# The queries' maxima over keys: four TensorE transposes, or VectorE's block transpose, one small TensorE transpose and a block diagonal from GpSimd

## The chip, the core and the metric

The kernel runs on one core of a Trainium2 chip. The metric is the device time of one launch in microseconds. The kernel before was run three times: 2422.80, 2423.19 and 2423.44 us, median 2423.19.

## The reference

Four sequences of 2048 tokens with 512 features, all in fp32, go through one layer: attention with one head of width 512, then a sparse feed-forward part.

```
q, k, v = relu(norm(x) @ Wq + bq), relu(norm(x) @ Wk + bk), relu(norm(x) @ Wv + bv)
e = q @ k.T / sqrt(512) - 10000 * (key is later than query)
e = exp(e - max(e, axis=keys))            # the maximum that this change is about
y = (e / sum(e, axis=keys)) @ v
x = x + norm(relu(y @ Wo + bo))
x = x + norm(feed_forward(norm(x)))       # top 32 of 512 outputs and of 512 inputs per token
```

## The kernel before

**Two phases.** Phase 1 is the attention, phase 2 the feed-forward part. Phase 1 works on groups of 512 queries (`GT`), four groups in each of four sequences, 16 in all, so that group `j` is group `j % 4` of its sequence. A group needs the keys of its own group and of those before it in the sequence. The program also holds a second form of both phases for inputs with large scores (`every_key=True`); with these inputs it isn't executed.

**Scores with keys on the partitions.** A score tile `st` holds 128 keys on its partitions and the group's 512 queries in its free dimension. `n.mx` (128 x 512, shown as `mxsum`) is the running maximum over all score tiles, made on VectorE by `combine` (line 227) as tiles come in. At the end `n.mx` still has 128 partial maxima for each query, one on each partition.

**The fold.** The maximum of each query over these 128 partitions must be found, and laid on every partition, since it is subtracted from score tiles that have keys on the partitions. Three functions do it:

- `fold` (713 to 718): four TensorE transposes of 128x128 put the queries on the partitions, in PSUM.
- `diagonals` (726 to 731): `reduced` (720 to 724) takes the maximum over the free dimension on VectorE, 128 queries x 4 tiles; then four VectorE scalings of the identity by one column each make four diagonal matrices, `n.dg`, 128 x 512.
- `spread` (733 to 736): a matmul of a matrix of ones with `n.dg` lays each query's maximum on all 128 partitions, `n.mb` in PSUM (128 x 512).

`weights` (738 to 752) then subtracts `n.mb` from each score tile (VectorE, 744), takes the exponential (ScalarE, 745) and adds up the tiles (GpSimd, 747 and 749). `attend` (774) multiplies the tiles with the values.

**The seven products.** Projections, and scores against the keys of earlier groups, are done as Strassen products of 2x2 blocks: class `Seven` (529), with the methods `p1` to `p7`, each four fp32 matmuls of 128x256 (line 561, two passes each in the profile). `p2`, `p3` and `p5` are copied out by ScalarE (580); `p1`, `p6` and `p7` leave a sum that VectorE evicts (609 and 613), and the next product of the same accumulator comes after that eviction. The letters name the target: `V`, `Q`, `K`, `O` for values, queries, keys and outputs of the next group, `A` and `N` for scores against earlier keys.

**The order of the work.** In phase 1 the order of the instructions on TensorE, VectorE and GpSimd is the order in which the program issues them; on ScalarE and SP (the DMA queue) it is left to the framework. TensorE's order is written out in `steps` (927). VectorE's jobs are put between TensorE's by the class `Pace` (229): it keeps an estimate of the time of TensorE (`pace.pe(us)`) and VectorE, and takes the next ready job from three ranks, lowest rank first; `pace.flush(job)` issues what is left of a job at once. The estimates only decide the order. Around the fold `steps` reads:

```
V.p3(), V.p6()
pace.flush(*n.maxima)
...
tp = fold(n.mx)
dg = pace.add(0, work(1.8, diagonals, n, tp))
pace.pe(0.45)
if last:
    next(filler), next(filler)
else:
    Q = Seven(nxt, "q")
    Q.p2(), Q.p5(), V.p7(), Q.p1(), V.p4()
pace.flush(dg)
spread(n)
```

In the last group there is no next one; its place is taken by `filler`, the products of `bound` (876 to 899, lines 886 and 898), which belong to a check on the size of the scores. The job list also holds `key_sums` (496), which stores key blocks by SP, `moments` (302), whose inverse root is GpSimd's (line 139), and `chain` (802), the norms of the group before.

**Buffers.** `n.dg` is a tile named `xn` of the pool `two`, which has two buffers for that name; `turn_x` (340) uses the same two later in the group. Weight loads go through a ring of 13 buffers (`Ring`, 357).

Of the kernel before, what the change touches and what calls it, by code (L numbers as in the profile page):

```python
# [28 lines left out]
F32 = mybir.dt.float32  # L29
# [3 lines left out]
ALU = mybir.AluOpType  # L33
AX = mybir.AxisListType
# [5 lines left out]
P = 128  # L40
GT = 512
TPG = GT // P
# [7 lines left out]
BLK = 32  # L50
# [3 lines left out]
def sandwich_kernel(ctx: ExitStack, tc: tile.TileContext, io: dict, out: bass.AP):  # L54
    nc = tc.nc
# [18 lines left out]
    ident = const.tile([P, P], F32, name="ident")  # L74
# [5 lines left out]
        out=causal, in_=causal, pattern=[[1, P]], compare_op=ALU.is_ge, fill=neg_raw, base=0, channel_multiplier=-1  # L80
    )
    ones = const.tile([P, P], F32, name="ones")
# [118 lines left out]
    def phase1(every_key):  # L201
# [8 lines left out]
        sm = enter("sm", 4)  # L210
        two = enter("two", 2)
# [70 lines left out]
        pace = Pace()  # L282
        ends = []

        def work(us, fn, *args, pause=0.0):

            fn(*args)
            yield us, pause
# [13 lines left out]
        def moments(n, joint=True):  # L302

            n.rstd = sm.tile([P, TPG], F32, name="rstd_x")
            var = sm.tile([P, TPG], F32, name="var_x")
            n.mv = sm.tile([P, TPG, nc.vector.BN_AGGR_DIM], F32, name="mv_x")
            for t, xt in enumerate(n.x):
                st = sm.tile([P, nc.vector.BN_STATS_DIM], F32, name="st_x")
                nc.vector.bn_stats(st, xt)
                nc.vector.bn_aggr(n.mv[:, t, :], st)  # L310
                if not joint:
                    nc.vector.tensor_scalar_add(var[:, t : t + 1], n.mv[:, t, 1:2], LN_EPS)
                    inv_sqrt(n.rstd[:, t : t + 1], var[:, t : t + 1])
                yield 0.8, 0.0
            if joint:
                nc.vector.tensor_scalar_add(var, n.mv[:, :, 1], LN_EPS)  # L316
                inv_sqrt(n.rstd, var)
                yield 0.2, (0.55,)
                n.shift = sm.tile([P, TPG], F32, name="shift_x")
                combine(n.shift, n.mv[:, :, 0], n.rstd, ALU.mult, -1.0)  # L320
                yield 0.2, 0.5

        def at_once(pieces):
            for _ in pieces:
                pass
# [14 lines left out]
        def turn_x(n):  # L340

            for t in range(TPG):
                xn = two.tile([P, D], F32, name="xn")
                nc.scalar.activation(
                    xn, n.x[t], AF.Identity, scale=n.rstd[:, t : t + 1], bias=n.shift[:, t : t + 1]
                )
                yield 0.0, 1.0
                nc.vector.transpose(n.x[t], xn)
                nc.sync.dma_start(xnT_d[n.i][t * P : (t + 1) * P, :], n.x[t])
                yield 0.65, 0.0  # L350
# [6 lines left out]
        class Ring:  # L357
# [36 lines left out]
            def drop(self, i):  # L394
                self.gone.add(i)
                self.fill()
# [313 lines left out]
            n.nk = GB * TPG if every_key else (n.g + 1) * TPG  # L710
            n.st, n.mx, n.maxima = [None] * n.nk, None, []

        def fold(src):

            tp = ps_tp.tile([P, NC, P], F32, name="tp")
            for t in range(TPG):
                nc.tensor.transpose(tp[:, t, :], src[:, t * P : (t + 1) * P], ident)
            return tp

        def reduced(tp, op):  # L720

            r = sm.tile([P, TPG], F32, name="fold")
            nc.vector.tensor_reduce(r, tp, axis=AX.X, op=op)
            return r

        def diagonals(n, tp):

            m = reduced(tp, ALU.max)
            n.dg = two.tile([P, TPG, P], F32, name="xn")
            for t in range(TPG):  # L730
                nc.vector.tensor_scalar_mul(n.dg[:, t, :], ident, m[:, t : t + 1])

        def spread(n):

            n.mb = ps_mm.tile([P, GT], F32, name="mm")
            nc.tensor.matmul(n.mb, lhsT=ones, rhs=n.dg.rearrange("p t q -> p (t q)"), start=True, stop=True)  # L736

        def weights(n):

# [136 lines left out]
        def bound():  # L876

            w = ring.take("q", range(NC))  # L880
            for d in range(NC):
                ps = ps_mm.tile([P, GT], F32, name="mm")

                cols = slice(d * P, D)
                for c in range(NC):
                    nc.tensor.matmul(
                        ps[:, cols],
                        lhsT=w[c][1][:, d * P : (d + 1) * P],
                        rhs=w[c][1][:, cols],
                        start=(c == 0),  # L890
                        stop=(c == NC - 1),
                    )
                    if c % 2:
                        pace.pe(0.43 * (NC - d))
                    if c == 1:
                        yield
                sqr = prp.tile([P, D], F32, name="pr")
                nc.scalar.activation(sqr[:, cols], ps[:, cols], AF.Square, accum_out=squared[:, 0, d : d + 1])
                yield
# [27 lines left out]
        def steps(n, ahead):  # L927
# [3 lines left out]
            for j in range(NGRP):  # L931
                nxt = ahead
                last = nxt is None
                filler = bound() if last else None
# [45 lines left out]
                else:  # L980
                    V = Seven(nxt, "v")
# [14 lines left out]
                stored = pace.add(1, key_sums(n)) if n.g < GB - 1 else None  # L996
                if ahead is not None:
                    measured = pace.add(1, moments(ahead), 2.0)
                tp = fold(n.mx)
                dg = pace.add(0, work(1.8, diagonals, n, tp))  # L1000
                pace.pe(0.45)
                if last:
                    next(filler), next(filler)
                else:
                    Q = Seven(nxt, "q")
                    Q.p2(), Q.p5(), V.p7(), Q.p1(), V.p4()
                pace.flush(dg)
                spread(n)
                pace.pe(0.86)
# [9 lines left out]
                if ahead is not None:  # L1019
                    pace.flush(measured)  # L1020
                    turned = pace.add(1, turn_x(ahead))
# [52 lines left out]
                before, n = n, nxt  # L1074
# [4 lines left out]
        n = load(*order[0], queues=(nc.sync, nc.sync if every_key else nc.scalar))  # L1079
# [15 lines left out]
        if every_key:  # L1095
            bo = broadcast(wp, "L0_attn_bo")
            for b in range(B):
                kTs, vos = [], []
                for g in range(GB):
                    if b + g:  # L1100
                        n = load(b, g)
                        at_once(moments(n))
                    transpose_x(n)
                    drop(project(n, "v"))
                    drop(project(n, "k"))
                    drop(project_vo(n))
                    kTs.append(n.kT)
                    vos.append(n.vo)
                for g in range(GB):
                    n = load(b, g)  # L1110
                    at_once(moments(n))
                    transpose_x(n)
                    drop(project(n, "q"))
                    no_scores(n)
                    for kt in range(n.nk):
                        score_tile(n, kt, kTs[kt // TPG])
                    diagonals(n, fold(n.mx))
                    spread(n)
                    at_once(weights(n))
                    inverses(n, summed(n.sum))  # L1120
                    n.a, n.xg, n.xr = [None] * TPG, [None] * TPG, [None] * TPG
                    for t in range(TPG):
                        load_residual(n, t)
                        attended(n, t, attend(n, t, vos))
                        at_once(chain(n, t))
                        if n.i == NGRP - 1 and t < TPG - 1:
                            features(n, t)
                    if n.i < NGRP - 1:
                        fetch_features(n.i)
                        pace.drain()  # L1130
            for br in branches:
                first_moments(n, br)
            ends.append(n.xg[TPG - 1])
        else:

            transpose_x(n)
            ahead = load(*order[1])
            at_once(moments(ahead))
            for m in "vqk":
                w = project(n, m)  # L1140
                weight_sums(m, w)
                if m == "k":
                    squares(w)
                drop(w)
            w = project_vo(n)
            ahead.ahead = [normed(ahead, t) for t in range(2)]
            weight_sums("o", w)
            drop(w)
            head.close()

            bo = broadcast(wp, "L0_attn_bo")
            for br in branches:
                nc.gpsimd.dma_start(
                    conv_w[br],
                    io[f"L0_ffn_{br}_conv_w"].rearrange("g f -> (g f)").rearrange("(o n) -> o n", o=1).broadcast_to((P, D)),
                )
            with tc.manual_schedule(engines={PE, mybir.EngineType.DVE, mybir.EngineType.Pool}):
                steps(n, ahead)
# [375 lines left out]
```

## Time and profile before

| | |
|---|---|
| median of three runs | 2423.19 us |
| the profiled execution, its time | 2423.45 us |
| its span in the profile | 2421.7 us |
| its granted TensorE clock | 0.996 |
| TensorE / VectorE / ScalarE / GpSimd busy | 98% / 74% / 46% / 38% |
| fold, TensorE transposes (717) | 64, 273 ns each |
| fold, VectorE reduction (723) | 16, 681 ns each |
| fold, VectorE scalings (731) | 64, 282 ns each |
| spread, TensorE matmul passes (736) | 32, 594 ns each |

A profile row names line, engine, operation, output<-input and shapes, the number of instructions, then their busy time and the mean of one, and the engine's idle time before them with what ended it. `PEld` is TensorE's weight load, which runs beside its matmuls. A matmul's duration in the profile includes its way through the array, so matmuls that follow each other overlap; what one costs in a stream is the distance from its start to the next one's.

### The profile page before, as it was taken

How to read it: one execution, taken by the hardware profiler on the slowest of the kernel's cores; microseconds unless marked ns; L12 is line 12 of the kernel's file. 1: busy time of each engine (PE TensorE's matmuls, PEld its weight loads, DVE VectorE, ACT ScalarE, POOL GpSimd, SP SyncE). 2: the span in 40 equal slices, each digit the busy share in tenths (PEclk: the TensorE clock that was granted, in tenths of full speed). 3: DMA queues.
4: the chain of work that ended last, by engine and by line, in shares of the span. 5: the costliest groups of instructions: out<-in, count | busy, mean ns of one | idle time of the engine just before them, and what ended most of it. 6: DMA issues, size and time to landing. Idle time of an engine off the chain costs nothing.

```text
span 2421.7 us, 29446 instructions
## 1 busy us (share of the span) xinstructions
PE 2368.4 (98%) x8418; PEld 1526.3 (63%) x8418; DVE 1788.8 (74%) x3879; ACT 1117.2 (46%) x2352; POOL 929.8 (38%) x875
## 2 busy tenths in 40 slices
PE   8999999999999999999999999999989999999997
PEld 3776858587685857768585776857434444444443
DVE  2588675558866565887656678655599999999997
ACT  2333423233442233343223334322268888888886
POOL 1012210311221031121203112120379999999997
PEclk9999999999999999999999999999999999999999
DMA  6587756568875656887565677734334444444441
GB/s 218 181 243 202 209 168 171 142 183 222 225 213 151 176 138 184 215 233 213 143 185 135 185 212 219 213 100 126 94 82 98 114 122 114 122 114 122 113 122 54
DMA packets 594735, 392.18 MB, mean 162 GB/s; under 512 B 393090, under 2 KB 460162, under 8 KB 594564
## 3 DMA queue, kind: packets, MB, share of 16 engines
q1 hardware_dynamic: 590932, 386.53, 57.6%
q10 hardware_dynamic: 3312, 2.63, 0.3%
q8 instruction: 70, 1.15, 0.2%
q0 software_dynamic: 320, 1.05, 0.2%
q14 instruction: 101, 0.83, 0.1%
HBM read 275.26 MB, written 114.82 MB: 161 GB/s over the span
## 4 chain that ended last, share of the span: by engine, by line
PE 73%; DVE 15%; ACT 4%; issue 4%; POOL 2%; DMA 1%; SPq 0%; POOLq 0%; ACTq 0%; DVEq 0%
PE acc L561 24%; PE acc L779 18%; PE mm L561 18%; PE mm L679 6%; DVE m_si L1246 4%; DVE m_so L1246 3%; DVE rest_so L1254 2%; DVE rest_si L1254 2%; PE mm L1325 2%; PE mm L414 2%; DVE rest_si L1257 1%; DVE rest_so L1257 1%; PE lg L1239 1%; PE mm L663 1%; PE mm L736 1%
## 5 line engine op out<-in xcount | busy, mean ns | idle before, releaser
L779 PE MATMUL acc<-vo,st 128*128 128x512 f32 x1088 | 476.0, 593 | 1.0 <-ACT st L745 1.0
L779 PEld LDWEIGHTS acc<-vo,st 128*128 128x128 f32 x1088 | 205.3, 190 | 240.4 <-issue 234.8
L1325 PE MATMUL mm<-w_L_ffn_weight,xsT 128*128 128x512 f32 x512 | 233.6, 599 | 4.1 <-ACT xsT L167 2.8
L1325 PE MATMUL mm<-w_L_ffn_weight,xnT 128*128 128x512 f32 x512 | 230.4, 592 | 1.7 <-ACT xnT L167 1.7
L139 POOL TENSOR_TENSOR rs_a<-ve_a,neg_half 128x1 f32<-128x1 f32 x64 | 44.5, 696 | 417.1 <-DVE ve_a L148 416.2
L1325 PEld LDWEIGHTS mm<-w_L_ffn_weight,xsT 128*128 128x128 f32 x512 | 98.0, 192 | 128.0 <-issue 116.2
L139 POOL TENSOR_TENSOR rstd_x<-var_x,neg_half 128x4 f32<-128x4 f32 (+1 forms) x19 | 17.8, 934 | 417.3 <-DVE var_x L316 412.7
L1325 PEld LDWEIGHTS mm<-w_L_ffn_weight,xnT 128*128 128x128 f32 x512 | 97.1, 190 | 122.9 <-issue 113.6
L561 PE MATMUL acc<-T,wb 128*128 128x256 f32 x720 | 170.2, 379 | 0.5 <-DVE qT L613 0.5
L561 PE MATMUL mm<-xnT,wb 128*128 128x256 f32 x720 | 170.1, 379 | 0.0
L749 POOL TENSOR_TENSOR mxsum<-mxsum,st 128x512 f32<-128x512 f32 (+2 forms) x144 | 162.3, 1127 | 14.6 <-ACT st L745 4.2
L561 PE MATMUL acc<-xnT,wb 128*128 128x256 f32 x720 | 165.2, 379 | 0.0
L561 PEld LDWEIGHTS acc<-T,wb 128*128 128x128 f32 x720 | 136.7, 190 | 25.9 <-issue 6.7
L561 PEld LDWEIGHTS acc<-xnT,wb 128*128 128x128 f32 x720 | 136.8, 190 | 25.0 <-issue 6.2
L561 PEld LDWEIGHTS mm<-xnT,wb 128*128 128x128 f32 x720 | 135.3, 190 | 24.0 <-issue 7.2
L679 PE MATMUL mm<-qT,kT 128*128 128x128 f32 (+3 forms) x512 | 148.6, 433 | 0.0
L227 DVE SCALAR_TENSOR_TENSOR mxsum<-mxsum,st 128x512 f32<-128x512 f32 (+2 forms) x144 | 86.5, 601 | 66.4 <-ACT st L607 61.7
L580 ACT COPY cp<-mm 128x512 f32<-128x512 f32 x72 | 42.1, 585 | 193.0 <-PE mm L561 191.8
L1246 DVE MAX8 m_si<-rest_si 128x8 f32<-128x512 f32 x192 | 129.9, 677 | 0.1
L1246 DVE MAX8 m_so<-rest_so 128x8 f32<-128x512 f32 x192 | 128.4, 669 | 0.1
L1254 DVE MATCH_REPLACE8 rest_si<-m_si,rest_si 128x512 f32<-128x512 f32 x192 | 128.4, 669 | 0.0
L1254 DVE MATCH_REPLACE8 rest_so<-m_so,rest_so 128x512 f32<-128x512 f32 x192 | 128.4, 669 | 0.0
(248 smaller groups left out, 4907.0 us busy)
## 6 DMA issues: line engine op xcount, KB each, us to landing
wb<-keys SPq DMA_DIRECT2D x168, 256.0 KB, 2.9
xr<-in_L_attn_x_dram SPq DMA_DIRECT2D x64, 256.0 KB, 3.8
x<-x SPq DMA_DIRECT2D x64, 256.0 KB, 3.1
xn<-xn SPq DMA_DIRECT2D x64, 256.0 KB, 2.9
out_dram<-h SPq DMA_DIRECT2D x64, 256.0 KB, 2.1
xt<-in_L_attn_x_dram SPq DMA_DIRECT2D x62, 256.0 KB, 3.3
wb<-Z_v SPq DMA_DIRECT2D x60, 256.0 KB, 2.9
wb<-Z_q SPq DMA_DIRECT2D x60, 256.0 KB, 3.3
```

Of the source, the lines that this page charges most:

```text
L139: nc.gpsimd.tensor_tensor(dst, src, neg_half[:, : src.shape[1]], ALU.pow)
L227: nc.vector.scalar_tensor_tensor(out, a, factor, b, ALU.mult, op)
L414: nc.tensor.matmul(ps, lhsT=w[c][1][:, d * P : (d + 1) * P], rhs=xnT[:, c, :], start=(c == 0), stop=(c == NC - 1))
L561: nc.tensor.matmul(ps[:, d * H : (d + 1) * H], lhsT=left[:, c, d * P : (d + 1) * P], rhs=right[:, c, :], start=(new and c + d == 0), stop= ...
L580: nc.scalar.copy(t, ps)
L679: nc.tensor.matmul(ps[:, off:], lhsT=kT[:, c, k : k + P], rhs=n.qT[:, c, off:], start=(c == 0), stop=(c == NC - 1),)
L749: nc.gpsimd.tensor_tensor(n.sum[:, off:], n.sum[:, off:], w, ALU.add)
L779: nc.tensor.matmul(acc, lhsT=n.st[kt][:, t * P : (t + 1) * P], rhs=vos[kt // TPG][:, kt % TPG, :], start=(kt == 0), stop=(kt == nk - 1),)
L1246: nc.vector.max(n.m8[br], n.rest[br] if k else n.lg[br])
L1254: nc.vector.match_replace(n.rest[br], n.m8[br], n.rest[br], -LOWEST)
L1257: nc.vector.match_replace(n.rest[br], n.m8[br], n.lg[br], -LOWEST)
L1325: nc.tensor.matmul(ps, lhsT=lhsT[:, c, :], rhs=wf[:, c, :], start=(c == 0), stop=(c == NC - 1))
```

## The change

The fold is done in four steps. VectorE transposes each 32x32 block of `n.mx` (`turned`), so that within each of the four block rows a partition stands for one query modulo 32, and 32 neighbouring elements are 32 keys' maxima for it. A VectorE reduction over these gives `n.m16`, 128 x 16. One TensorE transpose turns it to 16 x 128 in PSUM, a row for each block of 32 queries, and a second VectorE reduction over the four rows of blocks gives the maxima `m`, 16 x 32. GpSimd's select writes a 16 x 512 tile that has row `b`'s 32 maxima in columns `32 b` to `32 b + 31` and zeros elsewhere. The spread multiplies it with 16 rows of ones. In `steps` the first two steps are a job of their own; `Q.p2` (in the last group the first half of the filler) is issued before the TensorE transpose instead of after it, and the rest behind it.

```diff
-        def fold(src):
+        NB = GT // BLK
+
+        def block_maxima(n):
+
+            turned = two.tile([P, GT], F32, name="xn")
+            nc.vector.transpose(turned, n.mx)
+            n.m16 = sm.tile([P, NB], F32, name="m16")
+            nc.vector.tensor_reduce(n.m16, turned.rearrange("p (b k) -> p b k", k=BLK), axis=AX.X, op=ALU.max)
+
+        def fold(n):
 
             tp = ps_tp.tile([P, NC, P], F32, name="tp")
-            for t in range(TPG):
-                nc.tensor.transpose(tp[:, t, :], src[:, t * P : (t + 1) * P], ident)
-            return tp
-
-        def reduced(tp, op):
-
-            r = sm.tile([P, TPG], F32, name="fold")
-            nc.vector.tensor_reduce(r, tp, axis=AX.X, op=op)
-            return r
+            nc.tensor.transpose(tp[0:NB, 0, :], n.m16, ident)
+            return tp[0:NB, 0, :]
 
         def diagonals(n, tp):
 
-            m = reduced(tp, ALU.max)
-            n.dg = two.tile([P, TPG, P], F32, name="xn")
-            for t in range(TPG):
-                nc.vector.tensor_scalar_mul(n.dg[:, t, :], ident, m[:, t : t + 1])
+            m = sm.tile([NB, BLK], F32, name="m32")
+            nc.vector.tensor_reduce(m, tp.rearrange("b (i q) -> b q i", q=BLK), axis=AX.X, op=ALU.max)
+            n.dg = two.tile([P, GT], F32, name="xn")[0:NB, :]
+            nc.gpsimd.affine_select(
+                out=n.dg.rearrange("b (c q) -> b c q", q=BLK),
+                in_=m.unsqueeze(1).broadcast_to((NB, NB, BLK)),
+                pattern=[[1, NB], [0, BLK]],
+                compare_op=ALU.is_equal,
+                fill=0.0,
+                base=0,
+                channel_multiplier=-1,
+            )
 
         def spread(n):
 
             n.mb = ps_mm.tile([P, GT], F32, name="mm")
-            nc.tensor.matmul(n.mb, lhsT=ones, rhs=n.dg.rearrange("p t q -> p (t q)"), start=True, stop=True)
+            nc.tensor.matmul(n.mb, lhsT=ones[0:NB, :], rhs=n.dg, start=True, stop=True)
...
-                tp = fold(n.mx)
-                dg = pace.add(0, work(1.8, diagonals, n, tp))
-                pace.pe(0.45)
+                blocks = pace.add(0, work(1.4, block_maxima, n))
                 if last:
-                    next(filler), next(filler)
+                    next(filler)
                 else:
                     Q = Seven(nxt, "q")
-                    Q.p2(), Q.p5(), V.p7(), Q.p1(), V.p4()
+                    Q.p2()
+                pace.flush(blocks)
+                tp = fold(n)
+                dg = pace.add(0, work(0.3, diagonals, n, tp))
+                pace.pe(0.12)
+                if last:
+                    next(filler)
+                else:
+                    Q.p5(), V.p7(), Q.p1(), V.p4()
                 pace.flush(dg)
                 spread(n)
```

More of the change, by code (lines that the diff above doesn't have):

```diff
@@ L1116, in phase1 @@
                         score_tile(n, kt, kTs[kt // TPG])
-                    diagonals(n, fold(n.mx))
+                    block_maxima(n)
+                    diagonals(n, fold(n))
                     spread(n)
```

## The prediction

> **What bounds the kernel now.** I read the page first (busy shares, then the chain that ended last), then the windows, to see which stage the change lies in, then the timeline around one fold, then single rows for prices.
>
> ```profile
> PE 2368.4 (98%) x8418; PEld 1526.3 (63%) x8418; DVE 1788.8 (74%) x3879; ACT 1117.2 (46%) x2352; POOL 929.8 (38%) x875
> PE 73%; DVE 15%; ACT 4%; issue 4%; POOL 2%; DMA 1%; SPq 0%; POOLq 0%; ACTq 0%; DVEq 0%
> ```
>
> TensorE is busy for nearly the whole span, and most of the chain is its own matmuls. The next answer is the window of the sixteen attention groups.
>
> ```profile
> 80.00:1700.00 1620.00, 1617.27 (x6444) 1196.58 (x6443) 1079.23 (x2188) 546.54 (x1083) 294.21 (x313) 1.00 0.65 184
> ```
>
> In these 1620 us TensorE idles 2.7 us in all, VectorE 541 us, GpSimd 1326 us. So here a microsecond taken from TensorE's stream is a microsecond off the time, a microsecond in which it waits is one on it, and work of VectorE or GpSimd is free unless TensorE waits for it. All sixteen folds lie here (89.9 to 1686.4 us). One of them, group 3, in the timeline:
>
> ```profile
> 406.81 1.70 PEld L561 LDWEIGHTS acc<-T,wb 128*128 128x128 f32 x8
> 407.02 1.89 PE L561 MATMUL acc<-T,wb 128*128 128x256 f32 x8
> ...
> 408.54 0.58 PEld L717 LDWEIGHTS tp<-ident,mxsum 128*128 128x128 f32 x4
> 408.75 0.60 PE L717 MATMUL tp<-ident,mxsum 128*128 128x128 f32 x4
> ...
> 409.02 0.69 DVE L613 TENSOR_TENSOR vT<-acc,x 128x512 f32<-128x512 f32 x1 [2.76 <-PE acc L561]
> ...
> 409.19 1.89 PE L561 MATMUL mm<-xnT,wb 128*128 128x256 f32 x8
> 409.63 0.68 DVE L723 TENSOR_REDUCE fold<-tp 128x4 f32<-128x512 f32 x1
> ...
> 410.35 0.87 DVE L731 TENSOR_SCALAR xn<-ident,fold 128x128 f32<-128x128 f32 x4
> ...
> 411.14 0.68 DVE L309 BATCH_NORM_STATS2 st_x<-xt 128x6 f32<-128x512 f32 x1
> ```
>
> The line from 407.02 is V.p6. Call F the start of the first transpose, 408.75. The first matmul of Q.p2 starts at F+0.44, so four transposes take 0.44 us of the stream, 0.109 each (their 273 ns are latency); the eight passes of Q.p2 take 1.73, so Q.p5 starts at F+2.17. TensorE doesn't wait for the maxima: the last of them ended at F-3.1 here, and at F-1.1 or earlier in groups 0 to 14. VectorE takes V.p6's eviction (line 613) at F+0.27, since it must wait for V.p6, and only then what belongs to the fold. The same offsets return in groups 0 to 14; in group 1 the eviction starts at F+0.63.
>
> **The change, part by part.** The instruction order of the changed kernel on each engine is the old one but for the fold. TensorE: three transposes fewer in each of 16 groups, and the remaining one stands behind Q.p2. VectorE: the block transpose, the block reduction and the small reduction stand in one run where the reduction and the four scalings were, behind V.p6's eviction. GpSimd: one select more, before the moments' power. One pair also changes places: in group 1 a query eviction moves ahead of a product of the chain. ScalarE is unchanged; on SP a few stores of keys and loads of features change places with weight loads.
>
> TensorE's work: 3 x 0.109 = 0.33 us less a group, 5.2 us in 16 groups. The spread's matmul still has 512 columns in two passes, and I cost its 16 rows like 128: the 3-row matmul of line 1237 takes its 0.21 us a pass by its columns too.
>
> Here the Trainium skill differs from the row. "VectorE: DVE Perf Modes", section "The three transpose paths", gives 390 ns for TensorE's transpose of 128x128 and 311 ns for VectorE's blocks (in bf16), which makes four of the first worth 1.56 us and four of the second 1.24: the move would pay by itself, and three transposes less would give 16 x 1.17 = 18.7 us. In this trace a TensorE transpose in the stream is worth 0.109, four of them 0.44, and VectorE's block transpose of 128x512 takes 0.69. I use the trace: the gain is 5.2 us at most, and the maxima come later, not sooner.
>
> When the fold may start is the new wait. The prices:
>
> ```profile
> L835 DVE TENSOR_REDUCE xg<-pr 128x128 f32<-128x512 f32 x128 | 87.6, 685 | 3.7
> L348 DVE STREAM_TRANSPOSE xt<-xn 128x512 f32<-128x512 f32 x56 | 38.1, 692 | 1.9 <-ACT xn L344 1.9
> ```
>
> Same shapes as the new ones, so these are no bounds but values. Independent VectorE instructions of this size start 0.61 us apart (409.02 to 409.63), dependent ones 0.03 to 0.04 after the end before. So: eviction F+0.27, transpose F+0.88 to F+1.57, reduction F+1.61 to F+2.29. TensorE is through with Q.p2 at F+1.73: it has nothing to do for over half a microsecond. How soon it goes on is shown by a single transpose that waits for VectorE's reduction:
>
> ```profile
> 1750.56 0.69 DVE L835 TENSOR_REDUCE xg<-pr 128x128 f32<-128x512 f32 x1
> ...
> 1751.36 0.14 PEld L1338 LDWEIGHTS tp<-ident,xg 128*128 128x128 f32 x1 [1.18 <-issue]
> 1751.39 0.30 PE L1338 MATMUL tp<-ident,xg 128*128 128x128 f32 x1 [1.02 <-DVE xg L835]
> ...
> 1751.53 1.45 PE L1325 MATMUL mm<-w_L_ffn_weight,xnT 128*128 128x512 f32 x3
> ```
>
> The reduction ends at 1751.25, the weights load at 1751.36, the next matmul starts at 1751.53: 0.28 us from end to next matmul. The weight load after line 329 (ended 8.89, load at 8.95) came after 0.05 instead of 0.11, which would make it 0.22, and 16 stationary columns may load faster than 128. So Q.p5 starts between F+2.51 and F+2.57, against F+2.17 before: 0.34 to 0.40 us later a group. I take 0.37; outer bounds are 0.25 (columns that load in no time) and 0.55 (a semaphore more). The 0.33 saved is already in this, since Q.p2 now starts at F. Fifteen groups: 15 x 0.37 = 5.55 us.
>
> Group 1: its eviction is 0.36 later, so the fold is too (+0.36). The query eviction that moves ahead there ends a wait of 0.55 us, at 190.9, in which TensorE stood behind it (-0.55; nothing if it is late for another reason). Together -0.19.
>
> VectorE after the fold: the small reduction waits for TensorE's transpose, starting at about F+2.7. 128 elements a partition took 0.28 (line 731) and 0.29 from PSUM (line 1339), so it ends near F+3.0, and what is behind it in the queue (key sums or moments) starts at F+2.9 instead of F+2.39: 0.5 us late, while TensorE is 0.37 late. The first that TensorE needs from there is V.p7's eviction, before V.p4. VectorE was idle 0.82 us ahead of it (0.15 in groups 3, 7 and 11), and behind it there are 0.8 us until V.p4. So nothing further is late: cost zero, covered by that idle time; without it 0.15 us a group. Key stores that go out with this delay stand ahead of weight loads in SP's queue; TensorE waited for no load in this window and 13 buffers are in the ring: zero.
>
> GpSimd's select: the only rows are 128 elements.
>
> ```profile
> L79 POOL TENSOR_SCALAR_AFFINE_SELECT causal<-causal x1: 292/292/292, 1.4 to 1.4; 128x128 f32<-128x128 f32 x1
> ```
>
> For 512 it is between the 0.61 of a copy of 512 (line 747) and four times 292, 1.17 us; the operand read with stride zero is unlike any row. I take 0.85. It starts at F+3.1 and ends at F+4.0. The spread is due at F+9.4, behind Q.p5, V.p7, Q.p1 and V.p4: 5.4 us of cover, so zero in groups 0 to 14. Behind it on GpSimd is the moments' power, which isn't ready until later. It writes to the second of two buffers of that name, long free.
>
> Group 15 has no cover, only the filler. Before: last maximum 1685.66, scalings end 1688.39, spread 1688.54, then the subtractions, exponentials and the weighted sum, for which TensorE waits 1.0 us. After: transpose and reduction end at 1687.10, and half the filler (4 x 0.217 from 1686.15) at 1687.02, so the fold runs at once; transposed 1687.5, small reduction 1687.83, select from 1687.91 to 1688.76, spread at 1688.90. That is 0.36 later, between 0.1 and 0.7 for the bounds of the select.
>
> Sum: 5.55 - 0.19 + 0.36 = 5.7 us. The profiled execution took 2423.45 us (span 2421.7), the median is 2423.19, so the difference between them is nothing; 2423.19 + 5.7 = 2428.9, 0.24% slower.
>
> **The rivals.** A, as worked out: TensorE waits about 0.66 us for VectorE at each fold and keeps 0.33. Bounds of 0.25 and 0.55 a group, with the ends of groups 1 and 15, give +3.5 to +9 us.
>
> B, the cover holds: the block maxima are there when Q.p2 ends, and only the saving is left, 16 x 0.33 = 5.2 us: 2418. Its place is VectorE between V.p6 and the end of Q.p2; it decides for itself once the reduction ends before F+1.5, 0.8 us sooner than in my sum. For it speaks that the maxima are ready early (F-3.1) and that VectorE idles 2.76 us before the eviction; against it that the new instructions stand behind that eviction in the order, in every group.
>
> C, VectorE's second wait also hurts: if the small reduction resumes some 0.5 us later than I think, the idle time ahead of V.p7's eviction is used up and V.p4 waits as well, another 0.5 us a group: 2428.9 + 7.5 = 2436. The short idle of 0.15 us in groups 3, 7 and 11 speaks for it, the cover of 0.8 us behind it against.
>
> D, the select is a slow program on GpSimd with its broadcast operand: once it takes over 6 us the spread waits. At 8 us this would be 2 us a group, 2460. The 292 ns row speaks against it.
>
> **How the numbers follow.** A has 77%, B 8%, C 10%, D 5%. This kernel's measurement can tell 0.2% from no change, 4.85 us, so of A's chance about 57 points are slower and 20 within 0.2% (a step of under 0.31 us a group). Slower: 57 + 10 + 5 = 72%; within: 20%; faster: 8%, all of B. The range leaves out B, D and most of C: from 2426.0 to 2433.0, which A's bounds just fill.
>
> **What would show it.** The fold's transpose should have idle time of TensorE before it, put down to VectorE's block reduction, of 0.5 to 0.7 us in each of fifteen groups, some 10 us in all; the window's idle time of TensorE should rise from 2.7 to about 12 us, its work fall by 5. The block transpose should take 0.69, the reduction 0.68, the small one 0.28, the select 0.6 to 1.2, with no wait at the spread but in group 15; the wait at 190.9 should be gone. I am wrong if the fold doesn't wait, if V.p4 or the spread does, or if the distance from the reduction's end to Q.p5 isn't 0.2 to 0.3 us.

## The result and the profile after

The changed kernel takes 2433.35 us (median of five runs, 2432.87 to 2433.81), the kernel before 2422.96 in the same session (2422.74 to 2423.44): ratio 1.0042, 95% interval 1.0032 to 1.0053. It is slower by 10.4 us, nearly twice the 5.7 that was forecast, and just outside the forecast range. The profiled execution took 2432.98 us (span 2431.3, granted clock 0.996), so it stands for the median.

First the page's busy shares and chain, then the window of the attention groups (5 us longer than the one shown of before, since its last spread starts at 1699.7), then one row of TensorE's waits (time, times, longest).

```profile
PE 2371.8 (98%) x8370; PEld 1516.4 (62%) x8370; DVE 1798.3 (74%) x3847; ACT 1119.3 (46%) x2352; POOL 946.3 (39%) x891
PE 69%; DVE 17%; issue 6%; ACT 4%; POOL 2%; DMA 1%; SPq 0%; POOLq 0%; ACTq 0%; DVEq 0%
```

```profile
80.00:1705.00 1625.00, 1615.13 (x6373) 1183.59 (x6373) 1082.17 (x2144) 542.21 (x1071) 304.42 (x324) 1.00 0.65 184
```

```profile
PE tp L725 <- DVE m L720: 7.4, 15, 0.8
```

TensorE's idle time in the window is now 1625.00 - 1615.13 = 9.9 us instead of 2.7, and 7.4 us of it is one new wait: the fold's transpose for VectorE's block reduction, in fifteen groups. That is the wait that the prediction named. But the stage grew by more than its idle time did. From the spread of group 0 to that of group 14 it was 1467.22 us and is 1478.36: +11.14, while idle time rose by 7.1 and three transposes a group were saved. So TensorE lost time in places that no row calls idle. In the chain "issue", time without a visible wait, goes from 4% to 6% while PE falls from 73% to 69%; but 2% of the span is some 49 us, so these shares are no measure of the loss.

The fold of group 3 in the timeline. F, now the start of Q.p2, is 409.72:

```profile
409.72 1.89 PE L561 MATMUL mm<-xnT,wb 128*128 128x256 f32 x8
409.99 0.69 DVE L613 TENSOR_TENSOR vT<-acc,x 128x512 f32<-128x512 f32 x1 [2.75 <-PE acc L561]
410.60 0.70 DVE L718 STREAM_TRANSPOSE xn<-mxsum 128x512 f32<-128x512 f32 x1
411.33 0.69 DVE L720 TENSOR_REDUCE m<-xn 128x16 f32<-128x512 f32 x1
412.07 0.09 PEld L725 LDWEIGHTS tp<-ident,m 128*16 128x16 f32 x1 [0.87 <-DVE m L720]
412.08 0.28 PE L725 MATMUL tp<-ident,m 128*16 128x128 f32 x1 [0.47 <-DVE m L720]
412.19 1.95 PE L561 MATMUL mm<-T,wb 128*128 128x256 f32 x8
412.39 0.28 DVE L731 TENSOR_REDUCE m<-tp 16x32 f32<-16x128 f32 x1 [0.37 <-PE tp L725]
412.80 0.71 POOL L733 TENSOR_SCALAR_AFFINE_SELECT xn<-m 16x512 f32<-16x512 f32 x1 [45.06 <-DVE m L731]
```

VectorE runs eviction, block transpose and block reduction without a gap, and TensorE's transpose starts 0.06 us after the last of them. Q.p2's eight passes take 1.73 us of the stream and end at 411.45, so TensorE waits 0.63 us; the row says 0.47, since it counts from the modelled end of Q.p2's last pass (409.72 + 1.89). The second place to read has no idle time on PE at all: the spread of the same group. `PEld` is the weight load.

```profile
418.73 0.59 PE L561 MATMUL acc<-T,wb 128*128 128x256 f32 x2
419.25 0.29 PEld L746 LDWEIGHTS mm<-xn,ones 16*128 16x128 f32 x2 [0.33 <-issue]
419.25 1.12 PE L746 MATMUL mm<-xn,ones 16*128 16x512 f32 x2
420.30 0.73 PEld L561 LDWEIGHTS mm<-xnT,wb 128*128 128x128 f32 x4 [0.76 <-issue]
420.30 0.92 PE L561 MATMUL mm<-xnT,wb 128*128 128x256 f32 x3
```

And that spread before, with 128 rows:

```profile
417.61 0.41 PEld L736 LDWEIGHTS mm<-xn,ones 128*128 128x128 f32 x2
417.82 1.02 PE L736 MATMUL mm<-xn,ones 128*128 128x512 f32 x2
418.25 0.19 PEld L561 LDWEIGHTS mm<-xnT,wb 128*128 128x128 f32 x1 [0.24 <-issue]
418.68 0.81 PE L561 MATMUL mm<-xnT,wb 128*128 128x256 f32 x3
```

Before, the weights of the spread's ones are loaded 0.21 us ahead of its matmul, and those of the next product 0.43 ahead of theirs, behind running matmuls. After, each load starts together with the matmul that uses it. Durations say little of this (1.12 for 1.02); the starts do. From the last matmul before the spread to the second one behind it there are four distances: before 0.216 + 0.429 + 0.429 + 0.216 = 1.290 us, after 0.310 + 0.533 + 0.517 + 0.320 = 1.680. Each is about 0.1 us longer, 0.39 a spread, in all of groups 0 to 14.

### The profile page after: what moved, and what is told of

Read it like the earlier page. It is cut to its first block, busy times and chain, and to the rows that moved or that the text cites. A ratio compares the mean times of both kernels' runs of the same rounds, so it can differ in the third digit from the quotient of the medians.

```text
span 2431.3 us, 29370 instructions
## 1 busy us (share of the span) xinstructions
PE 2371.8 (98%) x8370; PEld 1516.4 (62%) x8370; DVE 1798.3 (74%) x3847; ACT 1119.3 (46%) x2352; POOL 946.3 (39%) x891
## 3 DMA queue, kind: packets, MB, share of 16 engines
q0 software_dynamic: 320, 1.05, 0.1%
## 4 chain that ended last, share of the span: by engine, by line
PE 69%; DVE 17%; issue 6%; ACT 4%; POOL 2%; DMA 1%; SPq 0%; POOLq 0%; ACTq 0%; DVEq 0%
PE acc L561 23%; PE acc L789 18%; PE mm L561 16%; PE mm L679 5%; DVE m_si L1263 4%; DVE m_so L1263 3%; DVE rest_so L1271 2%; DVE rest_si L1271 2%; PE mm L1342 2%; PE mm L414 2%; DVE rest_si L1274 1%; DVE rest_so L1274 1%; PE mm L746 1%; PE mm L663 1%; PE lg L1256 1%
## 5 line engine op out<-in xcount | busy, mean ns | idle before, releaser
L733 POOL TENSOR_SCALAR_AFFINE_SELECT xn<-m 16x512 f32<-16x512 f32 x16 | 15.5, 969 | 381.1 <-DVE m L731 381.1
```

## Experiments

My theory after reading the two traces: two costs of the same size, TensorE's wait at the fold (0.37 us a group, as forecast) and the 16-row spread (0.39 a group, forecast at nothing). The rivals: the whole difference belongs to the fold and what its delay does further on (a shifted VectorE and a shifted store order), and the spread's distances are only another view of it; or the spread is slower because GpSimd's tile or the new fold behind it is, and not because of its rows.

**All 128 rows in the spread, the rest as in the change.** The tile is zeroed ahead of time on GpSimd, and the select still writes 16 rows.

```diff
         def block_maxima(n):
...
+            n.dg = two.tile([P, GT], F32, name="xn")
+            nc.gpsimd.memset(n.dg, 0.0)
...
-            n.dg = two.tile([P, GT], F32, name="xn")[0:NB, :]
             nc.gpsimd.affine_select(
-                out=n.dg.rearrange("b (c q) -> b c q", q=BLK),
+                out=n.dg[0:NB, :].rearrange("b (c q) -> b c q", q=BLK),
...
-            nc.tensor.matmul(n.mb, lhsT=ones[0:NB, :], rhs=n.dg, start=True, stop=True)
+            nc.tensor.matmul(n.mb, lhsT=ones, rhs=n.dg, start=True, stop=True)
```

> The changed kernel, but the block diagonal is a tile of 128 rows, cleared by GpSimd ahead of the select, and the spread multiplies it with all 128 rows of ones. Theory (few rows cost): the spread's two passes and what follows them cost TensorE 0.39 us a group because weights of 16 rows are not loaded ahead of the matmul before them, nor the next full weights ahead of them; with 128 rows this goes, 16 x 0.39 = 6.2 us, so 2427.1 us, and the passes stand 0.43 us apart again. Rival 1 (late operand): the spread is slow because its operand comes from GpSimd; it stays slow, 2433.4 us or a little more for the clearing. Rival 2 (VectorE is late and holds TensorE elsewhere): also 2433.

Measured: 2425.93 us (2425.38 to 2426.78), ratio 1.0014 (1.0004 to 1.0023) beside 2422.66 before. That is 7.4 us less than the change, with more rows in the spread. Every spread of groups 0 to 14 is back at 1.290 us, and its loads run ahead again, as before; in group 3:

```profile
417.38 0.41 PEld L747 LDWEIGHTS mm<-xn,ones 128*128 128x128 f32 x2
417.59 1.02 PE L747 MATMUL mm<-xn,ones 128*128 128x512 f32 x2
418.02 0.19 PEld L561 LDWEIGHTS mm<-xnT,wb 128*128 128x128 f32 x1 [0.24 <-issue]
418.45 0.81 PE L561 MATMUL mm<-xnT,wb 128*128 128x256 f32 x3
```

The stretch from group 0's spread to group 14's is 1471.88 us, 6.5 below the change. The wait at the fold is still there. So the spread's rows are worth more than half of the loss, and the first rival is out.

**The fold of before, the spread with 16 rows.** This leaves out of what is subtracted the maxima of 112 in each 128 queries, so only its time counts.

```diff
-            nc.tensor.matmul(n.mb, lhsT=ones, rhs=n.dg.rearrange("p t q -> p (t q)"), start=True, stop=True)
+            nc.tensor.matmul(
+                n.mb, lhsT=ones[0:16, :], rhs=n.dg[0:16].rearrange("p t q -> p (t q)"), start=True, stop=True
+            )
```

> The kernel before with one edit: the spread uses only 16 of the 128 rows, so the maxima of 112 of each 128 queries are left out of what is subtracted. Few rows: the whole cost comes with it, 2423.0 + 16 x 0.39 = 2429.2 us. Late operand or VectorE: nothing in their way has changed, 2423.0 us.

Measured: 2429.94 us (2428.27 to 2431.55), ratio 1.0030 (1.0020 to 1.0040), +7.3 over before, with 1.680 us at every spread of groups 0 to 14; the stretch between the spreads is 1473.63 us, 6.4 above before. The rows alone, with no GpSimd select and no new fold, cost what the run above gave back; the second rival is out too. Its window from 80 to 1705 us shows how well this cost hides: 2.7 us of idle time, no more than before.

```profile
80.00:1705.00 1625.00, 1622.31 (x6435) 1193.20 (x6434) 1080.84 (x2186) 547.09 (x1082) 292.99 (x312) 1.00 0.64 184
```

**Rows by group: 16, 32, 64, 128, then 48, 65, 80, 96.** Two kernels, each with the zeroed tile of the first experiment and one size for each group of a sequence, so that one profile holds every size several times. Group 15, whose spread stands behind a wait, is left out of the distances.

```diff
-            nc.tensor.matmul(n.mb, lhsT=ones, rhs=n.dg, start=True, stop=True)
+            rows = (16, 32, 64, 128)[n.g]
+            nc.tensor.matmul(n.mb, lhsT=ones[0:rows, :], rhs=n.dg[0:rows, :], start=True, stop=True)
```

> As the kernel with 128 rows, but the spread uses 16, 32, 64 or 128 rows in groups 0, 1, 2 and 3 of each sequence, all with the same cleared tile. Few rows: the distance from the product before the spread to the second matmul behind it is 0.39 us longer with 16 rows than with 128; if the cost is one of any array form but the full one, 32 and 64 rows show the same 0.39; if it grows with the rows left empty, they lie between. Late operand: all four alike.

> As the kernel with rows by group, with 48, 65, 80 and 96 rows of the cleared tile in groups 0 to 3 of each sequence. Theory 1 (a change of the array's mode: the Trainium skill's page TensorEngine Tiling, Key Properties, says that changing the tiling mode drains TensorE, and it tiles rows for 64 and fewer): the 0.39 us come with 48 rows and are gone with 65, 80 and 96. Theory 2 (any number of rows but all 128 costs): 0.39 us with all four.

Measured (one run each): 2431.63 and 2428.41 us. The distance over the spread, by rows:

| rows | 16 | 32 | 48 | 64 | 65 | 80 | 96 | 128 |
|---|---|---|---|---|---|---|---|---|
| us | 1.680 | 1.680 | 1.681 | 1.681 | 1.296 | 1.296 | 1.296 | 1.290 |

It is a step between 64 and 65 rows, not a slope, as one theory had it for each of the two kernels. On both sides of it, in the second kernel:

```profile
528.31 0.29 PEld L748 LDWEIGHTS mm<-xn,ones 48*128 48x128 f32 x2 [0.33 <-issue]
528.31 1.12 PE L748 MATMUL mm<-xn,ones 48*128 48x512 f32 x2
```

```profile
609.26 0.41 PEld L748 LDWEIGHTS mm<-xn,ones 65*128 65x128 f32 x2
609.47 1.02 PE L748 MATMUL mm<-xn,ones 65*128 65x512 f32 x2
610.33 0.59 PE L561 MATMUL mm<-xnT,wb 128*128 128x256 f32 x2
```

With 48 rows load and matmul start together and the next matmul comes at 529.37, 1.05 us later; with 65 the load runs 0.21 ahead and the next comes after 0.86.

**The fold one product later, 16 rows.** To price the wait at the fold, the transpose goes behind Q.p5 instead of Q.p2.

```diff
-                    Q.p2()
+                    Q.p2(), Q.p5()
...
-                    Q.p5(), V.p7(), Q.p1(), V.p4()
+                    V.p7(), Q.p1(), V.p4()
```

> The changed kernel with the small transpose behind Q.p5 instead of Q.p2, so that the block maxima have 3.45 us of TensorE's work as cover instead of 1.73. Wait at the fold: its 0.47 us of idle time and the 0.06 behind it go, some 0.6 us a group in 15 groups, 9 us: 2424.4 us, the spread still slow. Rival 2 (VectorE is late): VectorE's small reduction comes later, so V.p4 waits for V.p7's eviction and the late query eviction of group 1 of each sequence waits longer; 2428 us or more.

Measured: 2422.71 us (2421.42 to 2423.34), ratio 1.000 (0.999 to 1.0009). 10.6 us less than the change: the wait is worth that much when it goes entirely, 0.37 of delay and 0.33 of saving, 0.70 a group (in the stretch between the spreads, now 1468.30 us, 10.1). The expectation asked for 1.7 us less of a gain. The fold's transpose now costs 0.325 us from the matmul before it to the one behind it, 0.216 for that matmul and 0.109 for itself: 16 stationary columns with 128 rows have no price of the spread's kind.

**Both: 128 rows, and the fold behind Q.p5.** The edits of the first experiment and of the last one together.

> Both corrections at once: a block diagonal of 128 rows for the spread, and the small transpose behind Q.p5. If the two costs are separate and complete, they add: the time with the small transpose behind Q.p5 (2422.7) less what 128 rows brought (2433.35 - 2425.93 = 7.4), 2415.3 us, with 5.2 us of that below the kernel before for three transposes less in each group. If they overlap (VectorE's lateness behind both), 2418 to 2422 us.

Measured: 2415.31 us (2414.82 to 2416.23), ratio 0.9970 (0.9958 to 0.9981) beside 2422.89 before. It beats both kernels, as expected. The fold of group 3:

```profile
407.23 0.69 DVE L720 TENSOR_REDUCE m<-xn 128x16 f32<-128x512 f32 x1
...
409.06 0.27 PE L727 MATMUL tp<-ident,m 128*16 128x128 f32 x1
...
409.17 0.60 PE L561 MATMUL acc<-xnT,wb 128*128 128x256 f32 x2
```

The reduction ends at 407.92, over a microsecond ahead of the transpose, and TensorE goes straight on. The stretch from group 0's spread to group 14's is 1461.84 us, 5.4 below before.

**128 rows, and the block transpose ahead of V.p6's eviction.** The other way to end the wait: the transpose stays behind Q.p2, but VectorE starts sooner.

```diff
-                    V.p3(), V.p6()
+                    V.p3()
+                    pace.flush(*n.maxima)
+                    blocks = pace.add(0, work(1.4, block_maxima, n))
+                    V.p6()
...
-                blocks = pace.add(0, work(1.4, block_maxima, n))
                 if last:
+                    blocks = pace.add(0, work(1.4, block_maxima, n))
```

> A block diagonal of 128 rows, the small transpose behind Q.p2 as in the change, but VectorE's block transpose and reduction issued before the eviction of V.p6 instead of behind it. Theory (the wait comes from VectorE's order alone, not from the length of its work): the idle time at the fold is gone in groups 0 and 2 to 14, 2415 to 2416 us; in group 1, where the last maximum is ready only 1.1 us before the old fold, some wait stays. Rival (the two instructions are too long for 1.73 us of cover wherever they stand, or they now hold V.p6's eviction up): a wait of 0.3 us or more stays in most groups, 2420 us or more.

Measured: 2417.47 us (2416.48 to 2418.16), ratio 0.9977 (0.9967 to 0.9986), 1.5 us above the upper end of what was expected.

```profile
405.05 0.69 DVE L720 TENSOR_REDUCE m<-xn 128x16 f32<-128x512 f32 x1
...
407.15 0.69 DVE L613 TENSOR_TENSOR vT<-acc,x 128x512 f32<-128x512 f32 x1 [1.42 <-PE acc L561]
...
408.61 0.27 PE L727 MATMUL tp<-ident,m 128*16 128x128 f32 x1
```

The reduction is ready 2.9 us ahead of its transpose, and no fold waits, not even in group 1, where I had expected some. So the cause of the wait was VectorE's order, the place behind the eviction. The stretch between the spreads is 1461.82 us, the same as with the fold behind Q.p5. The 2.2 us by which this kernel is slower than that one lie outside the stretch, about half ahead of it and half behind; why isn't settled.

## Why the prediction was right and where it was wrong

**The step that failed is a term of the sum**: "The spread's matmul still has 512 columns in two passes, and I cost its 16 rows like 128: the 3-row matmul of line 1237 takes its 0.21 us a pass by its columns too." Put at zero, it measured 0.39 us a spread in groups 0 to 14, 15 x 0.39 = 5.9 us; in group 15 the wait before the weighted sum gets shorter instead (0.80 us for 1.00). With it come three small waits that all the kernels with 16 or 32 rows in group 1 have and the others don't: in group 1 of the second to fourth sequence TensorE waits behind a late query eviction, 0.33 us each, 1.0 together. Between group 0's spread and group 14's this makes 14 x 0.39 + 1.0 = 6.5 us, and there the two runs on it gave 6.5 and 6.4. Their medians gave 7.4 and 7.3; what is above the sum lies outside that stretch (see the account).

The row was right and was misread. Its neighbours, in the profile of before:

```profile
1778.85 0.11 PEld L1237 LDWEIGHTS <-ones 3*128 3x128 bf16 x2 [0.17 <-issue]
1778.85 0.39 PE L1237 MATMUL lg<-lin_si,ones 3*128 3x512 bf16 x1
1779.08 0.37 PE L1237 MATMUL lg<-lin_so,ones 3*128 3x512 bf16 x1
...
1779.38 0.30 PEld L1239 LDWEIGHTS lg<-linT_si,xc_si 128*128 128x128 f32 x2 [0.42 <-issue]
1779.38 1.12 PE L1239 MATMUL lg<-linT_si,xc_si 128*128 128x512 f32 x2
```

The distance between the two 3-row matmuls is 0.23, close to the 0.21 that I took. But the first of them starts 0.205 us after the last transpose, where 0.109 is usual, and the next full-row matmul 0.30 after the second 3-row one: two changes of form, 0.10 us more on the way in and 0.08 on the way out. The type changes there as well, from fp32 to bf16 and back, so this row alone was a warning and no price. The weight loads show it too: both start with their matmul. In the changed kernel the spread stands alone between full-row matmuls, so it pays at both ends and between its own passes.

**The wait at the fold was right.** Forecast: Q.p5 later by 0.37 us a group; measured: 0.367 in groups 2 to 14. From the last matmul before the fold to the second behind it, 0.653 + 0.218 became 0.96 + 0.278. Eviction F+0.27, transpose F+0.88 to F+1.58, reduction F+1.61 to F+2.30 are as forecast; the next matmul comes at F+2.47 instead of 2.51 to 2.57, since the load of 16 columns follows the reduction after 0.05 and the next matmul follows the load after 0.12; and the second is late by another 0.06. So the 0.37 is 0.31 at Q.p5's first matmul, under the forecast's lower end of 0.34, and 0.06 at its second, of which the forecast knew nothing: that the size fits so well is luck. TensorE waits 0.63 us there (forecast: about 0.66). That the rows show 7.4 us of idle time and not "some 10" is their way of counting, from the modelled end: 0.47 a group.

**Group 1** was put at -0.19. The fold there costs +0.72 (the late eviction, as said), and this wait of the kernel before is gone:

```profile
190.92 0.92 PE L561 MATMUL acc<-T,wb 128*128 128x256 f32 x3 [0.55 <-DVE qT L613]
```

The row's 0.55, which the prediction took, counts from a modelled end again. By the starts the wait was worth 0.82: this matmul came 0.928 us after the one before it, and the next one 0.320 later; both distances are 0.216 in the changed kernel. Together -0.1. **Group 0** isn't like the others: its fold costs +0.48. **Group 15**: forecast +0.36; its fold waits 0.18 us, and the spread starts at F+2.48 instead of F+2.39, +0.1; the select took 0.71 us there, not 0.85, and TensorE waited 0.29 for it.

**VectorE and GpSimd behind the fold** cost nothing, as forecast. The small reduction takes 0.28. The select takes 1.05 us in most groups and 0.71 in groups 3, 7 and 11, inside the bounds of 0.61 to 1.17, and ends over 5 us ahead of the spread. So rivals C (a second wait of VectorE) and D (a slow select) didn't happen; nor B, since the block reduction ended at F+2.30 and not before F+1.5. The time came near C's 2436 for a reason that C doesn't have.

**The account.** In the stretch from group 0's spread to group 14's: fourteen spreads 14 x 0.39 = 5.46, three late query evictions 0.98, folds 13 x 0.367 + 0.72 = 5.49, the wait at 190.9 -0.82: 11.1 us, measured 11.14. Of the rest of the span's +9.6 us, 0.4 lies between group 14's spread and the last weighted sum, -0.4 ahead of the stretch (group 0's fold costs its 0.48 there, but the unedited start of the program varies by more: the first fold comes 0.8 us sooner in the old fold with 16 rows than in the kernel before), and -1.6 in what follows the last weighted sum, where the change edits nothing. That last part takes 680.23 us before, 678.66 after, and from 678.2 to 680.8 over all the profiles, and it doesn't follow the edits. What sets it wasn't tried and stays open; it is why the whole difference is smaller than the sum of the mechanisms.

## What to carry to other kernels

A lone matmul with 64 or fewer rows in a stream of full-row fp32 matmuls cost 0.39 us here, and zeros below its rows, up to 65 or more, made it free: shrinking the contraction to what is needed can be the dearer choice. Price such an edit by the distances between the starts of the matmuls around it, not by durations or idle time, both of which hide it. And when a step moves to another engine, look at what stands ahead of it in that engine's order: moving the waiting transpose behind one more product, or the block transpose ahead of the eviction, turned a loss into a gain.

## What the runs showed of the hardware

The step between 64 and 65 rows (1.68 and 1.30 us) is what the prediction lacked; ahead of the run with 65 rows it was one of two theories. The Trainium skill has a rule for it that the prediction had not weighed: "TensorEngine Tiling (Array Packing)", section "Key Properties", says that changing the tiling mode drains TensorE, and its section "Available Configurations" lists row tiling with tiles of 64 and of 32 rows, and nothing between 64 and all 128. The step's place agrees with it, and so does the loss of loads that run ahead: the 16-row load starts at 419.25, 0.07 before the modelled end of the full-row matmuls (418.73 + 0.59), and the next full-row load at 420.30, 0.07 before that of the spread.

There is a cost of 0.10 between the two passes of the spread as well, where no form changes. It is not the spread's own: the second matmul behind an ordinary wait is as late (0.320 for 0.216 us behind the one at 190.92), and so is the second pass of the full-row matmul behind the 3-row ones (0.533 for 0.429). So the four distances can be read as two breaks of the stream, one into the few rows and one out of them, each with a slow start behind it: 0.094 + 0.104 going in, 0.088 + 0.104 going out. No run takes these apart.

The same page lists tiles of 32 columns too. The fold's transpose, with 16 stationary columns and 128 rows, costs nothing extra when it needn't wait (0.325 = 0.216 + 0.109 us); no run has another matmul with so few columns in such a stream, so for those it stays open. That the engine changes a mode at all is the page's reading; the runs show the price, its step, and that this transpose doesn't have it.
